# Row scores of two graph attentions by way of DRAM instead of TensorE transposes, and three steps of the turn moved

## Chip, cores and metric

The kernel runs on one core of a Trainium2 chip. The metric is the device time of one execution in microseconds (us); the time before is the median of three runs.

The engines go by the profile's short names: PE is TensorE (PEld its weight loads), DVE is VectorE, ACT is ScalarE, POOL is GpSimd, and SP is SyncE, which only issues DMAs here.

## What is computed

64 graphs of 256 nodes with 256 features pass through two layers. The first is a graph attention applied twice, then a feed-forward; the second is an attention with eight heads, weighted by relation, then a feed-forward. In the inputs `adj` holds only 0 and 1.

```python
# layer 0, on x (64, 256, 256) and adj (64, 256, 256)
def _gat(h, adj, W, a, out_features):
    Wh = jnp.matmul(h, W)
    Wh1 = jnp.matmul(Wh, a[:out_features])          # one score per node
    Wh2 = jnp.matmul(Wh, a[out_features:])          # one score per node
    e = Wh1 + jnp.swapaxes(Wh2, 1, 2)               # column + row
    e = jax.nn.leaky_relu(e, negative_slope=ALPHA)
    scores = jnp.where(adj > 0, e, NEG)
    att = jax.nn.softmax(scores, axis=1)
    return jnp.matmul(att, Wh)

h = _gat(x, adj, W1, a1, Fout)
h = _gat(h, adj, W2, a2, W2.shape[1])
h = _layernorm(x + h, g_ln1, b_ln1)
x = _layernorm(h + relu(h @ w_ff1 + b_ff1) @ w_ff2 + b_ff2, g_ln2, b_ln2)

# layer 1, on that x
scores = jnp.einsum('bhid,bhjd->bhij', q, k) / np.sqrt(dh)
attn = jax.nn.softmax(scores, axis=-1)
for r in range(Wv.shape[0]):
    out = out + jnp.einsum('bhij,bhjd->bhid', attn * (adj == r)[:, None], v_r)
x = _ln(src + out @ Wo + bo, g1, beta1)
x = _ln(x + gelu(x @ W1 + b1) @ W2 + b2, g2, beta2)
```

In `_gat` the sum of a column and a row is taken: every node's second score has to lie along the free dimension and be the same on all partitions. How this row is made is the subject of the change.

## The kernel before

**Groups and turns.** Two graphs make a group, so there are 32 groups and T = 4 blocks of 128 nodes in each. A software pipeline works on three groups at once. `turn(y_, x_, z)` (L1275) takes group y through the attention with eight heads and its feed-forward, group x = y+1 through the first layer's feed-forward, and group z = y+2 through both graph attentions. There are 32 turns; z exists in the first 30.

**Order of the work.** Inside a turn with an x, a manual schedule covers PE, SP, DVE and ACT: each of these engines runs its instructions in the order in which the Python code issues them. POOL is left to the framework's scheduler. So moving a line of code moves its instructions in the queue of every engine that they belong to. Waits between engines and for free buffers are inserted by the framework.

**Score rows.** Each projected block of a group carries two extra columns with the two scores of its nodes (`xp`, columns F+2 and F+3, for the first graph attention; `hp`, columns F and F+1, for the second). `score_rows` (L777) takes a PSUM bank and fills it with four PE transposes of one column, broadcast to 128 columns; the result is a row of 512 scores on all 128 partitions. `Softmax.raw` (L797) adds row and column on ACT (L799), `leaky` is a DVE step (L807), `exp` is on ACT (L810), `masks` multiplies with the transposed adjacency on DVE and sums (L814).

**A turn, as far as it matters here.** In PE's order:

- projections, scores, exponentials and masks of y's four *quads* (a graph and half the heads each), mixed with the steps of x's hidden layer, which have names such as `3b`, `7b`, `sb`, `4b` (digit: one of seven products of a Strassen-like scheme; letter: half of the hidden blocks). `project(z, blocks)` is the first graph attention's projection (matmuls L772, copies to `xp` by ACT L774);
- `sums(2)` and `sums(3)`: the third and fourth quads' weighted sums (L1143) and the sums of their weights `zo` (L1146). For these DVE made totals in tiles with the tag `es`, of which there are two (L1133);
- `shares(1)`: DVE transposes `zo`, takes reciprocals and multiplies (L1154 to L1163; the result is `oT`, which has the buffer of `qk`);
- `out_(0)` and `out_(1)`: the output projection of y's two graphs (`yop`, L850, added by DVE in L853), then the layer norm's moments on DVE (L865, L866) after each;
- `out(1)`, `out(2)`, `out(5)`, ...: x's output product in seven parts (class `HiddenOut`, L1027, added by DVE in L1035). Four sums of quarters of the hidden layer, s1 to s4, are made by DVE in `sums` (L1013); parts 5, 6, 7 and 3 load s1, s2, s3 and s4 as PE weights. Among these parts stand z's first softmax, then its weighted sums (`hpp`, L839, copied to `hp` by ACT in L841);
- the second half: y's second hidden layer (`second`, L938), then y's output product with the same class and again the sums s1 to s4; among its parts stand z's second softmax and its weighted sums (`ygp`, L850).

**DMA queue.** SP issues, in its own order: the moves `hT<-yt` that finish transposed features (L726, L737), the loads of the next groups (`load_x` L436, `load_rows` L441, `load_adjacency` L449) and the stores of the result (L1243).

**Adjacency.** `early_adjacency(z)` (L1177) is one DVE transpose of 32 x 32 squares, 128 x 1024 int32 (L704), of data that the load has laid out for it.

Of the kernel before, what the change touches and what calls it, by code (L numbers as in the profile page):

```python
# [9 lines left out]
F32 = mybir.dt.float32  # L10
# [6 lines left out]
P = 128  # L17
# [368 lines left out]
def narrow_path(  # L386
# [13 lines left out]
    nc = tc.nc  # L400
    B, N, F = x.shape
# [7 lines left out]
    T = G * NB  # L409
    TN = G * N  # L410
# [6 lines left out]
    const = ctx.enter_context(tc.tile_pool(name="const", bufs=1))  # L417
    io = ctx.enter_context(tc.tile_pool(name="io", bufs=2))
    work = ctx.enter_context(tc.tile_pool(name="work", bufs=2))
    psum = ctx.enter_context(tc.tile_pool(name="psum", bufs=1, space=PSUM))  # L420
    ctx.enter_context(nc.allow_non_contiguous_dma(reason="vectors, once"))

    def bank(name):
        return psum.tile([P, 512], F32, tag="g", name=name, bufs=6)
# [258 lines left out]
    rows = work.tile([P, T, 2 * F], F32, tag="v", name="rows", bufs=1)  # L683
# [17 lines left out]
    def adjacency(u, aq):  # L701

        aT = work.tile([P, T, N], I32, tag="aT", name=f"aT{u}")
        nc.vector.transpose(aT.rearrange("p t n -> p (t n)"), aq.rearrange("p t n -> p (t n)"))  # L704
        return aT
# [60 lines left out]
    def projected(u, hT, blocks, xp):  # L766
        if xp is None:
            xp = work.tile([P, T, WX], F32, tag="wh", name=f"xp{u}")
        for t in blocks:
            ps = bank(f"xpp{u}_{t}")  # L770
            for k in range(KB):
                nc.tensor.matmul(ps[:, :WX], hT[k][:, t * P:(t + 1) * P], gwe[:, k, :],  # L772
                                 start=(k == 0), stop=(k == KB - 1))
            nc.scalar.copy(xp[:, t, :], ps[:, :WX])  # L774
        return xp

    def score_rows(u, l, wh, c):  # L777

        rows = bank(f"rows{u}_{l}")
        for t in range(T):  # L780
            nc.tensor.transpose(rows[:, t * P:(t + 1) * P],  # L781
                                wh[:, t, c:c + 1].to_broadcast([P, P]), ident)
        return rows

    class Softmax:
# [46 lines left out]
    def gat_first(u, s, xp, hp=None, blocks=range(T)):  # L832
        if hp is None:
            hp = work.tile([P, T, WX], F32, tag="wh", name=f"hp{u}")
        for t in blocks:
            b, i = divmod(t, NB)
            ps = bank(f"hpp{u}_{t}")
            for j in range(NB):
                nc.tensor.matmul(ps[:, :WH], s[:, b * NB + j, i * P:(i + 1) * P],  # L839
                                 xp[:, b * NB + j, :WH], start=(j == 0), stop=(j == NB - 1))  # L840
            nc.scalar.copy(hp[:, t, :WH], ps[:, :WH])  # L841
        return hp
# [54 lines left out]
    def affine(y, g_, b_):  # L897

        times(y, g_)
        plus(y, b_)  # L900

    def times(y, g_):
        nc.vector.tensor_mul(y, y, g_[:, None, :].to_broadcast(list(y.shape)))  # L903

    def plus(y, b_):
        nc.vector.tensor_add(y, y, b_[:, None, :].to_broadcast(list(y.shape)))  # L906
# [270 lines left out]
    def early_adjacency(z):  # L1177
        g[z]["aT"] = adjacency(z, g[z]["aq"])

    def project(z, blocks=range(T)):  # L1180
        d = g[z]
        d["xp"] = projected(z, d["xT"], blocks, d.get("xp"))

    def first_scores(z):
        d = g[z]
        d["m"] = Softmax(z, 0, d["xp"], score_rows(z, 0, d["xp"], F + 2), F + 3)

    def second_scores(z):
        d = g[z]
        d["m"] = Softmax(z, 1, d["hp"], score_rows(z, 1, d["hp"], F), F + 1)  # L1190

    def first_softmax(z):
        first_scores(z)
# [8 lines left out]
    def first_sums(z, blocks=range(T)):  # L1202
        d = g[z]
        d["hp"] = gat_first(z, d["m"].s, d["xp"], None if blocks[0] == 0 else d["hp"], blocks)
# [70 lines left out]
    def turn(y_, x_, z, rest=None):  # L1275
        Y, X, Z = (g.get(u) for u in (y_, x_, z))
        hT, y = Y["hT"], Y["y"]
        quads = [(b, m) for b in range(G) for m in range(KB)]
        p = Projections(y_, hT)
# [10 lines left out]
        def powers(n, heads):  # L1290
            exps(pe[n], *e[n], heads)
# [7 lines left out]
        def sums(n):  # L1299
            b, m = quads[n]  # L1300
            if m == 0:
                acc[b] = [psum.tile([P, 512], F32, tag=t_, name=f"{t_}{y_}_{b}") for t_ in ("po", "zo")]
            applied(b, m, v, *e.pop(n), *acc[b])
# [12 lines left out]
        def first(names):  # L1316
            steps(names)

        def moved(moves, n):
            for _ in range(n):  # L1320
                nc.scalar.copy(*next(moves))
# [3 lines left out]
        with order:  # L1325
# [27 lines left out]
            if X:  # L1353
                moved(moves, 2)
                p("q6")
                moved(moves, 1)
                p("v6")
                moved(moves, 3)
                times(X["y"], rg1)
                p("q3 q7 v7")  # L1360
                while late:
                    affine(*late.pop(0))
                p("v3 q4 v4")
                plus(X["y"], rb1)
                if waiting:
                    last = norm(w, 3, wy, mv=last)
                steps = first_hidden(x_)
                scores(0)
                scores(1, ())
                first("2a")  # L1370
                powers(1, (0, 1, 2))
                masks(0, (0,))
                if waiting:
                    offsets(*last)
                first("1a")
                masks(0, (2,))
                totals(0)
                first("5a")
                powers(1, (3,))
                first("2b 3a")  # L1380
                if waiting:
                    applied_norm(wy, *last, [0, 1])
                masks(1, (0,))
                first("6a")
                masks(1, (2,))
                totals(1)
                if waiting:
                    applied_norm(wy, *last, [2, 3])
                scores(2, ())
                sums(0)  # L1390
                powers(2, range(HPB))
                sums(1)
                first("ra")
                scores(3)
                masks(2, (0,))
                if Z:
                    early(z)
                shares(0, [0])
                if not y_:
                    with behind("low"):  # L1400
                        made(w1m, 2)
                first("7a sa 1b")
                shares(0, [1])
                masks(2, (2,))
                totals(2)
                first("5b 4a 6b 3b")
                masks(3, (0,))
                if Z:
                    project(z, range(0, 1))
                first("rb 7b")  # L1410
                if Z:
                    project(z, range(1, 2))
                first("sb")
                masks(3, (2,))
                totals(3)
                sums(2)
                sums(3)
                first("4b")
            else:
                powers(0, (1,))  # L1420
                p("q3 v3")
                powers(0, (2, 3))
                p("q6 v6 q7 v7")
                with behind("projected"):
                    masks(0)
                    totals(0)
                while late:
                    affine(*late.pop(0))
                p("q4 v4")
                scores(1)  # L1430
                masks(1)
                totals(1)
                sums(0)
                piece()
                scores(2)
                sums(1)
                piece()
                with behind("out"):
                    shares(0)
                masks(2)  # L1440
                totals(2)
                scores(3)
                piece()
                piece()
                masks(3)
                totals(3)
                sums(2)
                sums(3)
            if not Z:
                shares(1)  # L1450
            if X:
                out = HiddenOut(x_, 0, X["y"], X["h1"], wf2s, out_sums(x_, 0))
                if Z:
                    out.sums(1, 2)
            if Z:
                shares(1)
            if not y_:
# [7 lines left out]
                n = norm(y_, 2, y, range(NB))  # L1465
            piece()
            if Z:
                project(z, range(T // 2, T))
            if Z:
                early_adjacency(z)  # L1470
            elif X:
                out.sums(1)
                out(1, 2)
                out.sums(2)
            out_(1)
            piece()
            if Z:
                first_scores(z)
            if Z:
                n = norm(y_, 2, y, mv=mv)  # L1480
            else:
# [51 lines left out]
                n = moments(x_, 1, X["y"], range(NB))  # L1533
            if Z:
                first_sums(z, range(T // 2, T))
            if X:
                out.product(4)
            tt = work.tile([P, HPB, NB * N], F32, tag="e", name=f"tt{y_}_1")
# [39 lines left out]
            if y_ >= NG - 2:  # L1578
# [6 lines left out]
                    for _ in pieces:  # L1585
                        pass
                return
            second_scores(z)
            out = HiddenOut(y_, 1, y, h1, w2s, out_sums(y_, 1))
            out.product(1)  # L1590
            out.sums(1, 2)
# [191 lines left out]
    c = work.tile([P, 4], F32, tag="mv", name="checks")  # L1783
# [51 lines left out]
```

## Time and profile before

| | |
|---|---|
| median of three runs | 2951.56 us (2950.34 to 2952.9) |
| the profiled execution's own time | 2950.62 us |
| its span (first to last instruction) | 2949.0 us |
| granted TensorE clock | 0.998 |
| PE, PEld, DVE busy | 2921.7, 2505.9, 2611.3 us |
| ACT, POOL busy | 1897.2, 625.6 us |
| PE transposes of score rows in the turns and the set-up (L781) | 2 x 128, mean 0.273 and 0.278 us |
| DMA traffic | 34 GB/s mean |

How to read it: the profile is one execution, so durations from it are set against 2950.62 us. A turn with all three groups repeats every 89.97 us. Matmuls are pipelined, so the mean duration of a transpose (0.27 us) is longer than the step from one to the next (0.11 us). A bracket such as `[0.33 <-PE yf L1027]` gives the idle time of an engine ahead of an instruction and what ended it; `x16` says that so many instructions in a row are shown as one line.

### The profile page before, as it was taken

The page shows a single profiled execution, that of the slowest core. Times are in us where ns is not written, and L with a number is a line of the kernel's source. Part 1 is how long each engine was busy: PE and PEld are TensorE (multiplying, and loading weights), DVE is VectorE, ACT ScalarE, POOL GpSimd, SP SyncE. Part 2 cuts the span into 40 slices and gives each one's busy share as a digit, 9 for nine tenths or more (in the row PEclk, how much of TensorE's full clock was granted, in tenths as well). Part 3 has the DMA queues.
Part 4 walks back from the last instruction along what each step waited for, and adds up shares of the span by engine and source line. Part 5 has one row for each costly group of instructions (what it writes and reads, how often), then busy time and mean ns, then how long its engine had stood idle before and what let it go on. Part 6 is the DMA issues. An engine that isn't in the chain of part 4 may idle for free.

```text
span 2949.0 us, 58651 instructions
## 1 busy us (share of the span) xinstructions
PE 2921.7 (99%) x22206; PEld 2505.9 (85%) x22206; DVE 2611.3 (89%) x5028; ACT 1897.2 (64%) x3983; POOL 625.6 (21%) x931
## 2 busy tenths in 40 slices
PE   9999999999999999999999999999999999999997
PEld 7788888888888888888888888888888888888876
DVE  5889899989899889999898998899998989988887
ACT  5566666676676666666766766766667667667652
POOL 3312221122121122221221211222212212112211
PEclk9999999999999999999999999999999999999999
DMA  5011111111111111111111111111111111111000
GB/s 152 13 30 32 39 32 32 24 40 32 37 30 26 34 34 38 33 31 24 40 32 37 31 28 31 36 36 35 29 23 40 32 37 32 28 30 33 18 8 16
DMA packets 408020, 99.27 MB, mean 34 GB/s; under 512 B 357834, under 2 KB 407220, under 8 KB 407732
## 3 DMA queue, kind: packets, MB, share of 16 engines
q1 hardware_dynamic: 406332, 94.13, 14.8%
q8 instruction: 178, 2.92, 0.4%
q0 software_dynamic: 1056, 1.05, 0.1%
q14 instruction: 110, 0.90, 0.1%
q10 hardware_dynamic: 344, 0.28, 0.0%
HBM read 56.78 MB, written 16.78 MB: 25 GB/s over the span
## 4 chain that ended last, share of the span: by engine, by line
PE 97%; DVE 2%; ACT 1%; DMA 0%; issue 0%; POOL 0%; DVEq 0%; POOLq 0%; ACTq 0%
PE yf L1027 27%; PE h1a L938 15%; PE h1b L938 11%; PE po L1143 8%; PE v L1094 6%; PE qk L1094 6%; PE sp L1115 4%; PE hpp L839 4%; PE ygp L850 4%; PE xpp L772 4%; PE yop L850 4%; PE zo L1146 2%; PE rows L781 1%; DMA first<-in_adj_dram 0%; DVE st L865 0%
## 5 line engine op out<-in xcount | busy, mean ns | idle before, releaser
L1124 ACT ACTIVATE e<-sp 128x512 f32<-128x512 f32 x512 | 271.0, 611 | 71.2 <-issue 43.7
L1128 DVE TENSOR_TENSOR ea<-e,aT 128x1024 f32<-128x1024 f32 x256 | 311.1, 1217 | 1.6 <-ACT e L1124 1.6
L894 ACT ACTIVATE y<-y,nm,rs 128x256 f32<-128x256 f32 x442 | 235.1, 592 | 64.0 <-DVE nm L884 63.2
L947 DVE TENSOR_TENSOR h<-h1a,h 128x512 f32<-128x512 f32 x293 | 197.5, 682 | 81.7 <-PE h1a L938 78.5
L950 ACT COPY h<-h1b 128x512 f32<-128x512 f32 x293 | 175.2, 599 | 124.6 <-PE h1b L938 122.8
L956 ACT ACTIVATE h<-h,cols 128x256 f32<-128x256 f32 x512 | 221.9, 502 | 35.7 <-DVE h L947 31.5
L734 POOL COPY hT<-yt 32x256 f32<-32x256 f32 x244 | 211.3, 866 | 144.8 <-DVE yt L717 132.1
L1081 ACT COPY qk<-qk 128x512 f32<-128x512 f32 x128 | 74.3, 580 | 237.4 <-PE qk L1094 236.6
L865 DVE BATCH_NORM_STATS2 st<-y 128x6 f32<-128x256 f32 x512 | 208.7, 409 | 5.7
L876 POOL TENSOR_SCALAR rs<-mv 128x4 f32<-128x4 f32 (+1 forms) x134 | 41.7, 312 | 805.1 <-DVE mv L866 438.5
L1035 DVE TENSOR_TENSOR y<-yf,y 128x256 f32<-128x256 f32 x448 | 185.9, 415 | 29.8 <-PE yf L1027 29.8
L956 ACT ACTIVATE h<-h1a,cols 128x256 f32<-128x256 f32 x256 | 102.6, 465 | 131.9 <-PE h1a L938 131.9
L1156 POOL TENSOR_TENSOR low<-low,rq 128x16 f32<-128x16 f32 x64 | 13.9, 217 | 811.6 <-DVE rq L1155 811.6
L906 DVE TENSOR_TENSOR y<-y,rb 128x1024 f32<-128x1024 f32 x126 | 163.2, 1295 | 2.2
L1133 DVE TENSOR_TENSOR es<-e 128x1024 f32<-128x1024 f32 x128 | 156.0, 1219 | 0.0
L903 DVE TENSOR_TENSOR y<-y,rg 128x1024 f32<-128x1024 f32 x126 | 153.0, 1214 | 0.0
L877 POOL TENSOR_TENSOR rs<-rs,mhalf 128x4 f32<-128x4 f32 (+1 forms) x134 | 139.5, 1041 | 8.3
L1115 PE MATMUL sp<-qk 32*128 32x256 f32 x2048 | 138.4, 394 | 0.0
L938 PE MATMUL h1a<-tt,wf 128*128 128x256 f32 x512 | 137.7, 392 | 0.0
L1143 PE MATMUL po<-e,v 128*32 128x256 f32 x2048 | 135.5, 382 | 0.0
L1143 PE MATMUL po<-ea,v 128*32 128x256 f32 x2048 | 134.5, 379 | 0.0
L717 DVE STREAM_TRANSPOSE yt<-y 128x256 f32<-128x256 f32 x364 | 128.2, 407 | 0.9 <-ACT y L894 0.7
(288 smaller groups left out, 7738.4 us busy)
## 6 DMA issues: line engine op xcount, KB each, us to landing
hT<-yt SPq DMA_DIRECT2D x666, 32.0 KB, 1.8
y<-in_x_dram SPq DMA_DIRECT2D x32, 512.0 KB, 4.1
xq<-in_x_dram SPq DMA_DIRECT2D x240, 64.0 KB, 2.3
aq<-in_adj_dram SPq DMA_DIRECT2D x240, 64.0 KB, 2.3
out_dram<-y SPq DMA_DIRECT2D x30, 512.0 KB
wf<-in_L_gnn_w_ff_dram SPq DMA_DIRECT2D x2, 1024.0 KB, 7.8
w<-in_L_gnn_W_dram SPq DMA_DIRECT2D x2, 1024.0 KB
first<-in_adj_dram POOLq DMA_DIRECT2D x2, 512.0 KB, 9.0
```

Of the source, the lines that this page charges most:

```text
L734: nc.gpsimd.tensor_copy(to, at)
L850: nc.tensor.matmul(ps[:, i * F:(i + 1) * F], lhs(t, k), rhs(b, k), start=(k == 0), stop=(k == n - 1))
L865: nc.vector.bn_stats(st[:, t, :], y[:, t, :])
L894: mark["normed"] = nc.scalar.activation(y[:, t, :], y[:, t, :], AF.Identity, bias=nm[:, t:t + 1], scale=rs[:, t:t + 1])
L938: nc.tensor.matmul(ps[:, i * N:(i + 1) * N], w_[:, f * P:(f + 1) * P], m, start=first and i == 0, stop=True, skip_group_check=True)
L956: nc.scalar.activation(y, y if ps is None else ps[:, i * N:(i + 1) * N], func, bias=bi[:, f:f + 1])
L1027: nc.tensor.matmul(s.ps[n][:, i * F2:(i + 1) * F2], a[:, k, i * P:(i + 1) * P], w_[:, k, :], start=n in (1, 2, 5) and i == 0 and k == 0, s ...
L1094: nc.tensor.matmul(ps[:, i * N:(i + 1) * N], l, r, start=n in (1, 2, 5) and i == 0, stop=True, skip_group_check=True)
L1115: nc.tensor.matmul(ps[a][:, j * N:(j + 1) * N], k_[hp, m, j0:j0 + P], q[hp, m, b * N:(b + 1) * N], start=True, stop=True)
L1124: nc.scalar.activation(e[:, a, :], ps[a], AF.Exp, scale=isd)
L1128: nc.vector.tensor_tensor(ea[:, a:a + 2, :], e[:, a:a + 2, :], ab[:, None, :].to_broadcast([P, 2, NB * N]), ALU.mult)
L1143: nc.tensor.matmul(po[hp, m * N:(m + 1) * N], vs[:, hp], w[:, a, j * N:(j + 1) * N], start=(n == 0), stop=(n == len(terms) - 1))
```

## The change

- A new function `line_rows` writes the score column of all four blocks, 512 numbers, to a line in DRAM with one DMA, and reads the line back to all 128 partitions with a second one (256 KB into SBUF). Both are on SP's queue, and the second waits for the first. The tile has the tag `es`, which the totals of the exponentials and the reciprocals have too.
- Both softmaxes of the turns take their rows from there. The set-up in front of the turns, which handles groups 0 and 1, keeps `score_rows`.
- The first attention's projection is wholly ahead of `sums(2)`: blocks 0 and 1 where block 0 stood, blocks 2 and 3 where block 1 stood. Before, blocks 2 and 3 came between `out_(0)` and `out_(1)`.
- `early_adjacency` stands ahead of `sums(3)` rather than between `out_(0)` and `out_(1)`; on DVE that is between the totals of quad 3 and s1.
- Sum s2 of x's output product stands between `out_(0)` and `out_(1)` rather than right behind s1.

```diff
+    dram = ctx.enter_context(tc.tile_pool(name="dram", bufs=2, space=bass.MemoryType.DRAM))
...
+    def line_rows(u, l, wh, c):
+
+        line = dram.tile([T, P], F32, tag="line", name=f"line{u}_{l}")
+        rows = work.tile([P, TN], F32, tag="es", name=f"rows{u}_{l}")
+        nc.sync.dma_start(line.rearrange("t p -> p t"), wh[:, :, c])
+        nc.sync.dma_start(rows, bass.AP(tensor=line.tensor, offset=line.offset, ap=[[0, P], [1, TN]]))
         return rows
...
-    def first_scores(z):
+    def first_scores(z, rows=None):
         d = g[z]
-        d["m"] = Softmax(z, 0, d["xp"], score_rows(z, 0, d["xp"], F + 2), F + 3)
-
-    def second_scores(z):
+        d["m"] = Softmax(z, 0, d["xp"], score_rows(z, 0, d["xp"], F + 2) if rows is None else rows, F + 3)
+
+    def second_scores(z, rows=None):
         d = g[z]
-        d["m"] = Softmax(z, 1, d["hp"], score_rows(z, 1, d["hp"], F), F + 1)
+        d["m"] = Softmax(z, 1, d["hp"], score_rows(z, 1, d["hp"], F) if rows is None else rows, F + 1)
...
                 if Z:
-                    project(z, range(0, 1))
+                    project(z, range(0, 2))
                 first("rb 7b")
                 if Z:
-                    project(z, range(1, 2))
+                    project(z, range(2, T))
                 first("sb")
                 masks(3, (2,))
                 totals(3)
                 sums(2)
+                if Z:
+                    rows0 = line_rows(z, 0, Z["xp"], F + 2)
+                    early_adjacency(z)
                 sums(3)
                 first("4b")
...
                 if Z:
-                    out.sums(1, 2)
+                    out.sums(1)
...
             if Z:
-                project(z, range(T // 2, T))
-            if Z:
-                early_adjacency(z)
+                out.sums(2)
             elif X:
...
             if Z:
-                first_scores(z)
+                first_scores(z, rows0)
...
             if Z:
                 first_sums(z, range(T // 2, T))
+                rows1 = line_rows(z, 1, Z["hp"], F)
...
-            second_scores(z)
+            second_scores(z, rows1)
```

More of the change, by code (lines that the diff above doesn't have):

```diff
@@ L782, in score_rows @@
                                 wh[:, t, c:c + 1].to_broadcast([P, P]), ident)
+        return rows
+    def line_rows(u, l, wh, c):
[3 more added lines that the diff above has]
+        nc.sync.dma_start(rows, bass.AP(tensor=line.tensor, offset=line.offset, ap=[[0, P], [1, TN]]))
         return rows
```

## Prediction

> **What bounds the kernel now.** I read the page first, then the line that the change deletes, then one middle turn engine by engine in the timeline. The page:
>
> ```profile
> span 2949.0 us, 58651 instructions
> PE 2921.7 (99%) x22206; PEld 2505.9 (85%) x22206; DVE 2611.3 (89%) x5028; ACT 1897.2 (64%) x3983; POOL 625.6 (21%) x931
> ...
> PE 97%; DVE 2%; ACT 1%; DMA 0%; issue 0%; POOL 0%; DVEq 0%; POOLq 0%; ACTq 0%
> ```
>
> TensorE (PE) is never idle, so taking work from it looks like pure gain. But VectorE (DVE) is 89% busy, and a share over the span does not say how late DVE's results come. The timeline of PE's weight loads (start, duration, engine, line, count):
>
> ```profile
> 1511.53 0.57 PEld L781 LDWEIGHTS rows<-ident,hp 128*128 128x128 f32 x4
> 1512.07 1.87 PEld L1027 LDWEIGHTS yf<-w,h 128*128 128x128 f32 x16
> 1513.87 1.86 PEld L1027 LDWEIGHTS yf<-w2t,eq 128*128 128x128 f32 x16
> ...
> 1571.25 1.71 PEld L850 LDWEIGHTS yop<-wo,qk 128*128 128x128 f32 x8
> 1572.98 0.57 PEld L781 LDWEIGHTS rows<-ident,xp 128*128 128x128 f32 x4
> ...
> 1582.46 1.61 PEld L839 LDWEIGHTS hpp<-xp,s 128*128 128x128 f32 x8
> 1584.09 1.97 PEld L1027 LDWEIGHTS yf<-wf,eaq 128*128 128x128 f32 x16
> ```
>
> The L781 groups go away. What matters is what stands behind them: `yf<-w2t,eq` is product 5 of the second feed-forward's output and loads the sum s1 that DVE makes; `yf<-wf,eaq` at 1584.09 is product 7 of the first one's output and loads s3. DVE's timeline of the same turn:
>
> ```profile
> 1512.53 1.23 DVE L1013 TENSOR_TENSOR eq<-h 128x1024 f32<-128x1024 f32 x1 [1.58 <-ACT h L956]
> ...
> 1566.68 1.23 DVE L1013 TENSOR_TENSOR eq<-eq,h 128x1024 f32<-128x1024 f32 x1
> 1567.82 0.71 DVE L1154 STREAM_TRANSPOSE rz<-zo 128x512 f32<-128x512 f32 x1
> ...
> 1570.21 0.68 DVE L853 TENSOR_TENSOR y<-yop,y 128x512 f32<-128x512 f32 x1
> ...
> 1572.02 1.23 DVE L704 STREAM_TRANSPOSE aT<-aq 128x1024 int32<-128x1024 int32 x1
> 1573.40 0.69 DVE L853 TENSOR_TENSOR y<-yop,y 128x512 f32<-128x512 f32 x1 [0.16 <-PE yop L850]
> ...
> 1575.62 0.42 DVE L1035 TENSOR_TENSOR y<-yf,y 128x256 f32<-128x256 f32 x1 [0.33 <-PE yf L1027]
> ...
> 1582.25 1.36 DVE L1013 TENSOR_TENSOR eaq<-h 128x1024 f32<-128x1024 f32 x1
> ```
>
> Second half: s1 ends at 1512.53+1.23 = 1513.75 and its load starts at 1513.87, 0.115 later. Read over all 30 turns that have this pair, that distance is 0.114 to 0.125 us every time: PE is already only just waiting for DVE there. First half: s3 ends at 1582.25+1.36 = 1583.61, its load at 1584.09, 0.48 later in nearly every turn; less the 0.115 that a load needs after its sum, there are 0.37 us to spare. From 1570.21 to 1583.61 DVE has no idle time but the two brackets, 0.16 and 0.33 us. So PE and DVE are both critical in a turn of 89.97 us (1512.53 to 1602.49 for the same instruction).
>
> **What the Trainium skill says.** "Perfetto Trace Analysis", Optimization Strategy: a kernel can have regimes in which the most-contended engine changes; the trace agrees (above). "DMA: Bandwidth & Descriptors", Rules for kernel authors: a strided last dimension becomes one descriptor per element, so the line's write is 512 descriptors of 4 bytes; no transfer of before is that fine. Same page, Anatomy of one DMA: some 2.0 us fixed per DMA, mostly the write's receipt, longest to HBM. The DMA table agrees for what it has: 32 KB `hT<-yt` lands in 1.8 us, 64 KB `xq` in 2.3.
>
> **The change part by part, in that turn's times.**
>
> *Removed:* four transposes twice a turn. From the first to the next product PE takes 1573.63−1573.20 = 0.43 and 1512.18−1511.74 = 0.44 us; in 30 turns 26 us of PE time, the most that can be won. ScalarE's (ACT) eight reads of the scores come from SBUF instead of PSUM; I count that as nothing, within ±0.1 us a turn, hidden by ACT's idle 1.28 us before its exponentials.
>
> *Added:* two DMAs per attention on SP's queue. First attention: the last copy of the projection is done about 1564.8 (below). Write 1.8 us (nearest row) to 8.4 (estimate: 2 us plus 32 elements per DMA engine at 0.2 us of HBM access each, from the page's Latency and other measured facts); read of 256 KB 2.3 to 4.1 (64 and 512 KB rows). I take 5 together, so the rows are there at 1570. The deadline is about 1575.9, two score reads (0.83 us) before the leaky step at 1576.76 computed below: 11 us of room, upper end 12.5. In SP's queue the next work is the four `hT<-yt` issues at 1582.16; nothing waits behind. Second attention: the copies end at 1498.4, the write queues behind the 512 KB `y` load (4.1 us), rows at about 1508.4 (1499.3+4.1+5), needed at 1513.8; the twelve `hT<-yt` behind it start at 1508.64 and their product is used at 1521. All counted as nothing; late rows are a rival.
>
> *Moved, projection:* blocks 2 and 3 (1569.72 to 1571.47: 1.75 us) go ahead of the third quad's sums. Sums 2 and 3, 4b and the first `yop` group come 1.75 later; the second `yop` does not move. ACT's two extra copies delay its `sb` step from 1564.2 to about 1565.7, still ahead of s1 at 1566.7: nothing.
>
> *Moved, adjacency and s2:* they change places on DVE, 1.23 us each: nothing by itself.
>
> *What this does to DVE:* zo's last matmul ends at 1566.48+0.61 = 1567.09 now, 1568.84 then. DVE is through with s1 at 1567.9, as before, and now idles 1 us. Reciprocal and division run 1568.88 to 1571.35; the second `yop` load, due at 1571.25, waits to 1571.46 (+0.21). The first `yop` product ends at 1567.99+1.89+1.75 = 1571.63, so its addition starts at 1571.66 instead of 1570.21: 1.45 later. From there DVE is saturated. It took 1583.61−1570.21 = 13.40 before; the two idles (0.49) go, and 0.16 more, since an instruction that waits for nothing starts some 0.08 before its predecessor's end (1582.25 against 1581.94+0.39), at two places: 12.75. The leaky step comes 0.8 later (1575.96 to 1576.76) and s3 ends at 1571.66+12.75 = 1584.41. Product 7 can load at 1584.41+0.115 = 1584.52. Unhindered PE would be there at 1584.09−0.43+0.21 = 1583.87; it waits 0.65 and is **0.43 later than before**. Behind product 7 DVE has work that PE does not need at once, and idles 0.35 before the last addition (1589.82), so it catches up there.
>
> *Second half:* PE would reach product 5 at 1513.43, but s1's chain starts from the same PE products at the turn's middle (the h1a products from 1500.5 on) through additions, norm, transposes and eight ACT steps, none of them changed. It still arrives at 1513.75. PE waits 0.44: gain 0.
>
> *Sum:* 0.43 us × 30 turns = +13 us. Against the profiled execution's own 2950.62 us that is 2963.6; the median, 2951.56, is 0.94 above it, so 2964.5.
>
> **The rivals.**
> 1. *TensorE alone counts* (faster): both sums come early enough, perhaps since DVE's stretch packs tighter. For it: 99% busy PE and no wait in PE's list but 20 us, most at the ends. Against: the constant 0.115. It decides if s3 would end before 1583.5 and s1 before 1513.3. −26 us: 2925. If only the first half gains, −13: 2938.
> 2. *Break-even:* the stretch from the first `yop` addition to s3 shrinks by some 0.4 us more than I see, or PE's stages lose less between the merged groups. Second half 0, first half 0: 2951.
> 3. *Late rows* (slower still): the round trip by DRAM takes the upper 12.5 us, ready at 1577.3, against 1575.9: 1.4 us × 30 = 42 us on top of 13, 3006. It decides from 11 us on. Against: the DMA table has 32 and 64 KB landing in 1.8 and 2.3 us, in 128 B packets.
> 4. *Buffers:* the rows share the two `es` buffers with the exponentials' totals; if the reciprocal's tile must wait for the buffer of the rows (freed by ACT only after its score reads at about 1572), division comes 1 to 3 us late: 30 to 90 us, 2995. Against: with two in turn it gets that of the fourth total, freed by sums 3.
>
> **How the numbers follow.** Stated case 0.66; faster 0.12 (rival 1 and parts of it); break-even 0.14; late rows and buffers 0.08. ±0.2% (5.9 us) is about what a measurement of this kernel can tell from no change. The stated case's own range is 0.25 to 0.75 us a turn, 2958 to 2974: the overlap term may be missing (+0.16), or the score reads may let DVE start sooner. All of it is slower by over 0.2%, so slower is 0.74, same 0.14, faster 0.12. The range leaves out most of the faster cases and the late rows: 2947 to 2978.
>
> **What would show it.** Right: L781 left with only the 16 setup transposes; PE busy about 26 us less while the span grows; in PE's waits, `yf` waiting for DVE's `eq` 0.44 and for `eaq` 0.5 to 0.7 a turn, and `yop` for DVE's `qk` 0.2; `y<-yop` on DVE preceded by an idle ended by PE; the rows landing 4 to 8 us after their write is issued, ACT's L799 no longer waiting. Wrong: no wait of PE on those sums (rival 1), or ACT waiting for a DMA ahead of L799, and DVE for it at L807 (rival 3).

## Result, and the profile after

The changed kernel takes 3069.22 us (median of five runs, 3061.36 to 3073.61) against 2951.56: ratio 1.0393, 95% interval 1.0381 to 1.0404. Slower, as forecast, but by 118 us where 13 were forecast. The profiled execution took 3070.37 us with a clock of 0.987, and the mean turn 93.65 us instead of 89.97: 110 us in 30 turns. Another 8.7 us lie ahead of the first turn with a z (121.9 us instead of 113.2), where PE ran 20.5 us at half clock instead of 3.4. How long that stretch is differs between executions (23.9 us in the profiled ones of e1_moves_only and e5_packed, 3.4 in most others) and moves a time by up to 10 us, so small differences are read below from the turns.

From the page of the kernel after (span, busy times, the shares of the chain that ended last):

```profile
span 3068.5 us, 58409 instructions
PE 2953.9 (96%) x21966; PEld 2506.9 (82%) x21966; DVE 2606.9 (85%) x5028; ACT 1905.4 (62%) x3983; POOL 621.0 (20%) x931
...
PE 71%; DVE 10%; DMA 9%; ACT 5%; issue 2%; POOL 1%; SPq 1%; DVEq 0%; ACTq 0%; POOLq 0%
```

PE had been the whole chain (97%); now DMA, DVE and ACT hold a quarter of it. PE has 240 matmuls less and is busy for longer: at half clock, at the start and in the places shown below, the same matmuls take longer. The waits, one view for each engine (us in total, times, longest), first ACT's and DVE's, then SP's queue and PE's:

```profile
ACT s L808 <- DMA rows<-line: 234.1, 43, 8.5
...
DVE s L816 <- ACT s L808: 82.0, 43, 3.5
```

```profile
SPq L791 <- DMA line<-hp: 265.7, 30, 10.6
SPq L791 <- DMA line<-xp: 243.5, 29, 10.3
```

```profile
PE yf L1036 <- DVE y L1044: 83.4, 43, 3.7
PE yf L1036 <- DVE eq L1022: 6.2, 30, 0.2
```

This is one chain read backwards. PE waits for an addition of DVE, DVE's leaky step (L816, formerly L807) for ACT's score reads, ACT for the row, and the read of the row (L791) for its own write, some 9 us each time. Not every microsecond counts: of ACT's 234 us most fell into time in which it had nothing due, and 82 reached DVE.

Before, DVE's only idle times in the same stretch of a turn were 0.16 and 0.33 us. Here is one turn of the kernel after, in the order of the chain. First SP's queue (start, duration, what is issued):

```profile
1636.39 0.38 SPq L790 DMA_DIRECT2D line<-xp  x1
1644.82 0.35 SPq L791 DMA_DIRECT2D rows<-line  x1
...
1664.87 0.36 SPq L790 DMA_DIRECT2D line<-hp  x1
1674.64 0.34 SPq L791 DMA_DIRECT2D rows<-line  x1
```

From the issue of the write to that of its read 1644.82−1636.39 = 8.43 us passed. ACT's and DVE's timelines:

```profile
1649.67 1.71 ACT L808 ACTIVATE s<-rows,xp 128x256 f32<-128x256 f32 x4 [7.33 <-DMA rows<-line]
...
1678.79 1.31 ACT L808 ACTIVATE s<-rows,hp 128x256 f32<-128x256 f32 x3 [0.57 <-DMA rows<-line]
```

```profile
1650.61 1.49 DVE L816 SCALAR_TENSOR_TENSOR s<-s 128x512 f32<-128x512 f32 x2 [2.25 <-ACT s L808]
```

The score reads start 4.85 us after the read's issue and 13.28 us after the write's. DVE stood idle for 2.25 us ahead of the leaky step. PE, in an earlier turn and then at product 5 of the second half:

```profile
1554.26 3.74 PE L1036 MATMUL yf<-wf2t,eq 128*128 128x128 f32 x32
1560.61 2.74 PE L1036 MATMUL yf<-wf,eaq 128*128 128x128 f32 x16 [2.62 <-DVE y L1044]
...
1565.91 1.95 PE L1036 MATMUL yf<-wf,eaq 128*128 128x128 f32 x16
```

```profile
1678.18 2.02 PE L1036 MATMUL yf<-w2t,eq 128*128 128x128 f32 x16 [0.20 <-DVE eq L1022]
```

The product at 1560.61 is product 3 of the first half. It uses the PSUM bank of product 5, and so waits until DVE has added product 5, which stands behind the leaky step in DVE's queue. Its 16 matmuls take 2.74 us, those at 1565.91 take 1.95. The granted clock of three neighbouring stretches shows why (bounds, length, busy time of PE and the others, PEclk):

```profile
1558.38:1561.79 3.41, 1.18 (x10) 1.18 (x11) 3.38 (x15) 2.65 (x6) 0.20 (x1) 1.00 0.00 0
1561.79:1565.20 3.41, 3.41 (x13) 3.04 (x13) 3.41 (x7) 3.34 (x9) 2.23 (x3) 0.50 0.07 19
1565.20:1568.61 3.41, 3.41 (x25) 3.16 (x25) 2.64 (x4) 3.31 (x8) 2.18 (x2) 1.00 0.22 72
```

Around such a wait the trace grants half the clock for 3.413 us, in 14 of the 30 turns with a z; the kernel before has this in none of them (each of the two has one more behind them). "TensorE: Matmul & The Clock Gate", Part 1 of the Trainium skill, describes this: a gate that halves the clock after an idle window of about 3.4 us and counts in windows of 3413 ns. The length agrees to the nanosecond, and the starts of the 14 lie whole multiples of it apart. The idle time doesn't agree: PE's waits were shorter, 2.3 to 2.9 us in 13 of the 14. What separates the turns in this trace is how a wait lies to these windows. In the window ahead of each of the 14, PE was idle for 2.02 us or more (3.41−1.18 = 2.23 in the one shown); in no other window of the turns was it idle for more than 1.94, though the other 16 turns have waits of 2.1 to 3.5 us too. The same holds for the 13 intervals in the turns of e3_line_first below (1.98 or more, and 1.94). Behind the last of these turns three intervals, in e7_packed_s2 and e10_both, follow 1.6 to 1.9 us of idle time, so this bound is not the whole rule.

### The profile page after: what moved, and what is told of

It is laid out like the page before. It is cut to its first block, busy times and chain, and to the rows that moved or that the text cites. A ratio compares the mean times of both kernels' runs of the same rounds, so it can differ in the third digit from the quotient of the medians.

```text
span 3068.5 us, 58409 instructions
## 1 busy us (share of the span) xinstructions
PE 2953.9 (96%) x21966; PEld 2506.9 (82%) x21966; DVE 2606.9 (85%) x5028; ACT 1905.4 (62%) x3983; POOL 621.0 (20%) x931
## 4 chain that ended last, share of the span: by engine, by line
PE 71%; DVE 10%; DMA 9%; ACT 5%; issue 2%; POOL 1%; SPq 1%; DVEq 0%; ACTq 0%; POOLq 0%
PE yf L1036 16%; PE h1a L947 9%; PE h1b L947 8%; PE v L1103 6%; PE qk L1103 6%; PE po L1152 6%; DMA rows<-line 5%; PE sp L1124 4%; PE hpp L848 4%; DMA line<-xp 4%; PE xpp L773 4%; PE ygp L859 4%; ACT h L965 2%; PE yop L859 2%; ACT s L808 2%
## 5 line engine op out<-in xcount | busy, mean ns | idle before, releaser
L1036 PE MATMUL yf<-wf,eaq 128*128 128x128 f32 x1024 | 143.3, 299 | 78.5 <-DVE y L1044 78.4
L1036 PEld LDWEIGHTS yf<-wf,eaq 128*128 128x128 f32 x1024 | 132.8, 208 | 92.0 <-DVE y L1044 84.3
L808 ACT ACTIVATE s<-rows,xp 128x256 f32<-128x256 f32 x128 | 54.3, 496 | 222.0 <-DMA rows<-line 221.7
L816 DVE SCALAR_TENSOR_TENSOR s<-s 128x512 f32<-128x512 f32 x128 | 87.9, 688 | 85.4 <-ACT s L808 82.0
```

The costliest lines, as they stand in the source:

```text
L1036: nc.tensor.matmul(s.ps[n][:, i * F2:(i + 1) * F2], a[:, k, i * P:(i + 1) * P], w_[:, k, :], start=n in (1, 2, 5) and i == 0 and k == 0, s ...
```

## Experiments

Comparisons are with the kernel before on the same chip. Turns are medians over a profiled execution, counted from DVE's transpose of x for the group z (`xT<-xq`, L1174 before). "First" and "second" mean the two graph attentions of a turn, or the half of a turn that holds each; the second half begins with PE's first matmul of y's second hidden layer (`h1b<-hT,w`, L938 before). Where the rows are late, turns differ from each other by up to 3 us, and the median tells less than the mean.

| kernel | first row | second row | median us | ratio, 95% interval | turn us |
|---|---|---|---|---|---|
| before | PE | PE | 2951.56 | 1 | 89.97 |
| after | line | line | 3069.22 | 1.0393 [1.0381, 1.0404] | 93.76 |
| e1_moves_only | PE | PE | 2959.25 | 1.0025 [1.0016, 1.0035] | 90.17 |
| e2_line_second | PE | line | 2979.97 | 1.0096 [1.0073, 1.0120] | 90.95 |
| e3_line_first | line | PE | 3054.60 | 1.0355 [1.0326, 1.0384] | 92.97 |
| e4_no_write | read only | read only | 2961.31 | 1.0031 [1.0018, 1.0043] | 90.17 |
| e5_packed | packed line | packed line | 2975.48 | 1.0059 [1.0036, 1.0081] | 90.39 |
| e7_packed_s2 | packed line | packed line | 2956.60 | 1.0017 [1.0007, 1.0026] | 90.02 |
| e8_packed_s2_split | packed line | packed line | 2960.35 | 1.0024 [1.0016, 1.0033] | 90.14 |
| e9_first_hoisted | packed line | PE | 2973.89 | 1.0085 [1.0069, 1.0101] | 90.57 |
| e10_both | packed line | line, early | 2972.38 | 1.0063 [1.0046, 1.0081] | 90.42 |
| e12_dense_second | PE | line, early | 2943.01 | 0.9971 [0.9961, 0.9981] | 89.56 |
| e11_packed_dense | packed line | line, early | 2937.92 | 0.9954 [0.9936, 0.9971] | 89.40 |

### Which part costs what

**e1_moves_only:** the moves stay, both rows come from PE again (against the kernel after).

```diff
-                    rows0 = line_rows(z, 0, Z["xp"], F + 2)
...
-                first_scores(z, rows0)
+                first_scores(z)
...
-                rows1 = line_rows(z, 1, Z["hp"], F)
...
-            second_scores(z, rows1)
+            second_scores(z)
```

> The changed kernel with both row scores made by TensorE transposes again; the three moved steps stay moved. Theory (the round trip through DRAM costs most, the moves cost VectorE's shorter cover): 0.43 us a turn, about 2964 us, TensorE waits some 0.2 us a turn for s3 and none for the leaky step. Rival (the moves cost it all): about 3069 us. Second rival (the moves cost nothing by themselves): 2951 us.

**e2_line_second** makes the first pair of these edits alone, **e3_line_first** the second pair alone:

```diff
 # e2
-                    rows0 = line_rows(z, 0, Z["xp"], F + 2)
-                first_scores(z, rows0)
+                first_scores(z)
 # e3
-                rows1 = line_rows(z, 1, Z["hp"], F)
-            second_scores(z, rows1)
+            second_scores(z)
```

> The changed kernel with the first attention's rows by TensorE again, the second's by the line in DRAM. Theory: 2964 us from the moves, and a late row in about half of the turns at the second attention, 0.3 to 0.5 us a turn on average, so 2970 to 2980 us; no half-speed intervals of TensorE's clock. Rival (both attentions share the loss equally): about 3015 us.

> The changed kernel with the second attention's rows by TensorE again, the first's by the line. Theory: the first attention carries nearly all of the loss: some 2.7 us a turn, and another 1.5 us in about half of the turns by a lower clock after the long wait, 3045 to 3060 us. Rival (equal shares): about 3015 us.

**e4_no_write** keeps the reads and drops the writes: the row is a piece of the input x, so the scores are other numbers, and nothing waits for a landing.

```diff
-        nc.sync.dma_start(line.rearrange("t p -> p t"), wh[:, :, c])
-        nc.sync.dma_start(rows, bass.AP(tensor=line.tensor, offset=line.offset, ap=[[0, P], [1, TN]]))
+        src = x[0:1, 0:2].rearrange("b n f -> (b n f)")
+        nc.sync.dma_start(rows, bass.AP(tensor=src.tensor, offset=src.offset, ap=[[0, P], [1, TN]]))
```

> The changed kernel without the write of the line: both rows are read by the same 256 KB transfer from a fixed line of the input x, so the scores' row part is other data and nothing waits for a write. Theory: the read alone lands in about 5 us, well ahead of its use, and what is left is the moves' cost less nothing: the sum of the prediction, about 2964 us, with waits for s1 of 0.4 us and for s3 of 0.6 us a turn, and the full clock. Rival (the read's 256 KB, or traffic on the DMA rings, costs too): above 2985 us. Rival (TensorE alone counts once the rows are early): 2925 us.

Measured side by side, with the kernel before at 2952.69: the moves cost 2959.25−2952.69 = 6.6 us, the first line 3054.60−2959.25 = 95.4, the second 2979.97−2959.25 = 20.7. Together these are 123, against 118 for the whole change. They don't simply add: in e2 the second half is 0.67 us longer than before in the mean (53.53 against 52.86), in the kernel after only 0.26, and the kernel after has its long start besides. Since e4 stands where e1 stands (both turns 90.17), what comes on top of the moves goes with the write and the wait for it; reading the rows from SBUF and the buffers of tag `es` cost nothing that shows.

PE's waits, e3 and then e4:

```profile
PE yf L1036 <- DVE y L1044: 83.2, 36, 3.4
```

```profile
PE yf L1035 <- DVE y L1043: 6.6, 7, 2.6
PE yf L1035 <- DVE eq L1021: 6.5, 30, 0.5
```

The second line of e4 is the wait of product 5 for s1 in the second half: once in each of 30 turns, with the transposes gone and no row late. Product 5 ends where it ended before (16.27 us after the middle of the turn, 16.26 before). This is why the second half gains nothing.

The first line's 95 us can be taken apart by turns. In the 17 turns of e3 without a half-speed interval the first half is 39.94 us long in the mean, against 37.33 in e1: 2.6 us for the late row, 78 us in 30 turns. In the 13 turns with one it is 41.34, 1.40 us more, 18 us in all. PE waits nearly as long in both kinds of turns (2.7 us in the mean, and 2.6), so that nearly all of the 1.40 us goes with the clock and not with a later row.

### Why the write takes 9 us

**e5_packed:** GpSimd first gathers the column into a tile of its own, so that each partition's four scores are one piece of 16 bytes: 128 pieces instead of 512. The row then lies node by node, and ACT reads every fourth number.

```diff
-        line = dram.tile([T, P], F32, tag="line", name=f"line{u}_{l}")
+        col = work.tile([P, T], F32, tag="col", name=f"col{u}_{l}")
+        line = dram.tile([P, T], F32, tag="line", name=f"line{u}_{l}")
...
-        nc.sync.dma_start(line.rearrange("t p -> p t"), wh[:, :, c])
+        nc.gpsimd.tensor_copy(col, wh[:, :, c])
+        nc.sync.dma_start(line, col)
...
-        return rows
+        return rows.rearrange("q (p t) -> q t p", t=T)
...
```

> The changed kernel, but the scores are first gathered by GpSimd into a tile of 128 x 4 and the line is written in 128 pieces of 16 bytes instead of 512 of 4 bytes; the row is read back as before and ScalarE takes it with a stride. Theory (the write's receipts come back one after another, per piece): the write lands in about 3 us instead of 8 to 10, both rows are in time, and the kernel is where the one without a write was, about 2961 us. Rival (a fixed price of a write to DRAM, whatever its pieces): still 8 us or more, above 3030 us.

**e6_probe:** the kernel before with an extra write and a small read behind it in each turn, which no other work waits for; four kinds in turn: 512 pieces of 4 bytes side by side (S = 1) or 512 bytes apart (S = P), 128 pieces of 16 bytes, 128 of 512 bytes.

```diff
...
+            S = (1, P)[kind]
+            line = dram.tile([T, P, S], F32, tag=f"line{S}", name=f"probe{kind}_{z}")
+            nc.sync.dma_start(line.rearrange("t p s -> p t s")[:, :, 0], g[z]["hp"][:, :, F])
+            nc.sync.dma_start(back[:, 0:1], line[0:1, 0, 0:1])
...
+            line = dram.tile([P, T], F32, tag="line", name=f"probe{kind}_{z}")
...
+            line = dram.tile([P, P], F32, tag="lines", name=f"probe{kind}_{z}")
...
```

> The kernel before with one extra write to DRAM a turn behind the second score column, whose landing a small read on the same queue waits for; its form changes from turn to turn: 512 pieces of 4 bytes side by side, 512 pieces of 4 bytes at 512 bytes from each other, 128 pieces of 16 bytes, 128 pieces of 512 bytes. Theory (receipts in turn, per piece): 8 to 10 us for both forms of 512 pieces, about 3 to 4 us for both forms of 128. Rival (pieces that share a memory line wait for each other): 8 to 10 us only for those side by side, and more than 4 for 128 pieces of 16 bytes. Rival (a piece below 512 bytes costs a read first): 128 of 512 bytes about 2 us, 128 of 16 bytes clearly more.

The probe left the kernel's time as it was: 2953.35 us in its one run, with turns of 89.97.

SP's waits in the probe; the first line holds both kinds of 4-byte pieces:

```profile
SPq L431 <- DMA probe<-hp: 83.8, 14, 10.2
SPq L435 <- DMA probe<-mhalf: 25.8, 8, 3.8
SPq L439 <- DMA probe<-ident: 24.0, 8, 3.3
```

Taken apart by kind, from the issue of the write to that of the read: 512 pieces of 4 bytes side by side 8.8 to 10.7 us; 512 such pieces at a spacing of 512 bytes 3.7 to 4.0; 128 of 16 bytes 3.6 to 4.3; 128 of 512 bytes 2.6 to 3.9. All four were issued 0.4 to 0.6 us behind y's load of 512 KB, so the three shorter times may be this load's as much as their own. The theory that each small piece costs its own receipt falls: the same 512 pieces, spaced, land in less than half the time. For pieces of 4 bytes it counts that they lie side by side. The 16-byte pieces lie side by side too and are not slow, which the rival had not expected (more than 4 us); whether their size or their smaller number helps them was not tried. "DMA: Bandwidth & Descriptors", Specifications, of the Trainium skill says that transfers below 512 bytes are read-modify-write; pieces that share the same 512 bytes would then have to follow one another, 128 of them in the 4-byte line and 32 in the 16-byte line. That is a guess which fits the probe; no run here shows it.

In e5 the lines land in time (write to read 1.7 us in the first half, median), and the first half is as long as e4's. Yet e5's profiled execution is 16 us longer than e4's (2976.24 against 2960.22). Its longer stretch at half clock at the start is 10 of these; what remains is the price of the strided read. Score reads, e5 and then the kernel after (busy, mean ns of one):

```profile
L811 ACT ACTIVATE s<-rows,hp 128x256 f32<-128x256 f32 x120 | 82.5, 770 | 0.0
L811 ACT ACTIVATE s<-rows,xp 128x256 f32<-128x256 f32 x120 | 81.9, 755 | 20.6 <-DMA rows<-line 20.6
```

```profile
L808 ACT ACTIVATE s<-rows,xp 128x256 f32<-128x256 f32 x128 | 54.3, 496 | 222.0 <-DMA rows<-line 221.7 <-PE rows L782 0.3
```

That is a quarter of a microsecond more for each of eight reads in a turn; the second half is 0.22 us longer than e4's, 7 us in 30 turns.

### Can the moves and the second half be made to pay?

**e7_packed_s2:** as e5, with s2 of x's product back behind s1.

```diff
-                    out.sums(1)
+                    out.sums(1, 2)
...
-            if Z:
-                out.sums(2)
-            elif X:
+            if not Z and X:
```

> As the packed version, with s2 back behind s1 ahead of the reciprocals, so that VectorE does it in the idle time in front of zo. Theory: VectorE's stretch behind the first yop product is 1.14 us shorter, the wait for s3 goes and the first half gains 0.3 to 0.44 us a turn against before; the second half still waits for s1: about 2940 us (2937 to 2944). Rival (zo is not what VectorE waits for, or another wait takes its place): 2952 us or more.

DVE then makes s2 in the 1 us in which it waits for `zo`. The forecast of 2940 us was missed. The first half is 36.98 us against 37.33 in e5 and 37.13 before: a gain at last, but of 0.15 us rather than the transposes' 0.43; the second `yop` group now starts 0.21 us later than before, behind the division, which takes most of the rest. The second half gives 0.2 back.

**e8_packed_s2_split:** s1 of the second half also in two pieces, so that product 5 starts on the first.

```diff
...
+                if n == 1 and split:
+                    for k in (slice(0, 2), slice(2, 4)):
+                        mark["quarters"] = nc.vector.tensor_tensor(o[:, k], x_[:, k], y_[:, k], op)
+                    continue
...
-            out.sums(1, 2)
+            out.sums(1, split=True)
+            out.sums(2)
```

> As the one with s2 ahead, and the second feed-forward's s1 made in two halves, of which the first needs only the first half of ScalarE's steps, so that its last part ends some 0.5 us earlier. Theory (the second half waits for s1 alone): both deletions of transposes now count, 0.8 us a turn, about 2928 us (2924 to 2934). Rival (another chain of the second half is as long): no better than the one without the split, about 2940 us.

The forecast of 2928 us was missed too. The wait for s1 is gone and another has its place, at product 7 (PE's timeline):

```profile
1526.91 2.05 PE L1047 MATMUL yf<-w,eaq 128*128 128x128 f32 x16 [0.38 <-DVE y L1055]
```

By the timelines, ACT's strided reads (2.75 us for four) make DVE's leaky step late, and with it the addition of product 6, whose bank product 7 takes.

**e9_first_hoisted:** e7's first half with x's product 1, its addition, z's score reads and exponentials moved up between the two `yop` groups; the second row from PE.

```diff
             if Z:
-                out.sums(2)
+                first_scores(z, rows0)
+                out(1)
+                Z["m"].scores(0)
...
             out_(1)
...
```

> The first attention by the line in 16-byte pieces with s2 ahead of the reciprocals; the second by TensorE's transposes as before; and x's first output product with its addition, and z's leaky steps and exponentials, between the two yop groups, so that the second yop group does not wait for the division. Theory: the first half now shows the deleted 0.43 us in full, the second half is that of before: about 2940 us. Rival (VectorE's stretch is as long as TensorE's, since the moments of the second graph come later): 2948 us or more.

The forecast of 2940 us was missed by 34. Compared with e7, the second `yop` group starts 1.57 us later, behind the product that was moved ahead of it (20.76 us after the turn's start instead of 19.19). Its addition follows at 22.69, and everything behind it on DVE: s3 ends at 32.26 instead of 30.97.

**e10_both:** e9's first half; in the second the 4-byte line of the changed kernel, but written ahead of y's load on SP's queue and read behind it, with s1 in two pieces.

```diff
-                rows1 = line_rows(z, 1, Z["hp"], F)
+                read1 = dense_rows(z, 1, Z["hp"], F)
+                if z + 1 < NG:
+                    load_rows(z + 1)
+                rows1 = read1()
```

> As the one before, and the second attention by a line of 4-byte pieces too, whose write is issued ahead of the load of y so that its row comes without a stride and in time (13.5 us after the write, with some 15 us of room), and s1 of the second feed-forward in two halves. Theory (in the second half only s1, late rows and the slow strided read stood in the way): another 0.4 us a turn, about 2928 us. Rival (the row is late, or the next chain, the addition ahead of part 7, holds TensorE): no better than without, 2940 us or more.

The whole disappoints as e9 does, but from the middle of the turn to the next turn's start it needs 0.33 us less than the kernel before (median). So its second half was put behind other first halves: **e12_dense_second** behind that of before, **e11_packed_dense** behind that of e7 (edits as in e10 and e7, without e9's).

```diff
 # e11 and e12, second half
+                read1 = dense_rows(z, 1, Z["hp"], F)
+                if z + 1 < NG:
+                    load_rows(z + 1)
+                rows1 = read1()
...
+            out.sums(1, split=True)
 # e11 alone, first half
+                    rows0 = line_rows(z, 0, Z["xp"], F + 2)
...
+                    out.sums(1, 2)
```

> First half as before (x's rows transposed, nothing moved), second half as e10_both alone. If the second half gains 0.36 us by itself: turn 89.6 us, 30 x 0.36 = 11 us under before, 2941 us, ratio 0.9963. If that gain was borrowed from e10_both's first half: turn 90.0 us, 2952 us, ratio 1.000. If the line is late, over 91 us a turn and over 2980 us.

> First half of the turn as e7_packed_s2 (x's rows by the packed line, s2 ahead of the reciprocals, nothing hoisted), second half as e10_both (hp's rows by 512 pieces of 4 bytes, written ahead of y's load, s1 in two halves). If the halves add: turn 90.0 - 0.15 (first half of e7_packed_s2 against before) - 0.36 (second half of e10_both against before) = 89.46 us, some 15 us less than before over 30 turns, 2937 us, ratio 0.995. The rival, that the shorter second half was only e10_both's own first half paying back (work that lay ahead there), gives a second half like e7_packed_s2's or before's: turn 89.8 to 90.0, 2948 to 2956 us. If hp's line lands later than its read is wanted, as in the kernel after: a turn over 91 us and over 2980 us.

Both gains stood, and by the turns they added. The second half takes 89.56−37.13 = 52.43 us in e12 and 89.40−36.98 = 52.42 in e11, against 52.84 in the kernel before and in e4: 0.41 of the 0.44 us of the transposes. SP's queue in e12:

```profile
1493.57 0.39 SPq L800 DMA_DIRECT2D dense<-hp  x1
1494.49 0.37 SPq L442 DMA_DIRECT2D y<-in_x_dram  x1
1503.93 0.34 SPq L803 DMA_DIRECT2D rows<-dense  x1
```

The write still takes 8.3 to 11.4 us. It is issued 0.4 us after the start of the last copy of `hp` instead of 1.7 (medians), and the score reads wait at most 0.16 us for the row. So it is the lateness of the row that costs, not the write itself or SP's queue standing behind it. PE's timeline no longer has a bracket at product 5:

```profile
1506.84 1.95 PE L1059 MATMUL yf<-w,h 128*128 128x128 f32 x16
1508.62 1.95 PE L1059 MATMUL yf<-w2t,eq 128*128 128x128 f32 x16
```

And the page of e11, to be set beside that of before: PE's busy time is 16.5 us less, and the span 12.6.

```profile
span 2936.4 us, 58412 instructions
PE 2905.2 (99%) x21966; PEld 2475.9 (84%) x21966; DVE 2616.5 (89%) x5058; ACT 1931.4 (66%) x3983; POOL 662.6 (23%) x961
```

e11, at 2937.92 us, beats both kernels, the one before by 0.5%. The split alone, with the transposes kept, was not run; at product 5 it has nothing to take away, since the matmuls of product 5 start 1.78 us after those of product 1 before as well as in e12 (in e4, which waits, 2.16).

## Why the prediction was right or wrong

**The step that failed** is *Added*: "I take 5 together". The working gave the write 1.8 to 8.4 us, and the sum took the low end, from transfers of 128-byte packets. Measured for the first line: 8.5 us for the write (median, 8.2 to 10.8) and about 5 for the read, 13.3 from the issue of the write to the first score read. The deadline that the text had worked out, 11 us of room, held: 13.3−11 = 2.3 us late, and e3's first halves without a half-speed interval are 2.3 (shortest) to 2.6 us (mean) longer than e1's. The right arithmetic was there with the wrong value in it; rival 3 was what happened, with the sign that the text had named for it (ACT waiting for a DMA, and DVE for ACT), and the chance of 0.08 that it shared with the buffers was an error of the same step.

**Luck.** That the kernel became slower was forecast, but for a reason that makes up 6.6 of the 118 us; that both reasons point the same way is luck. And the upper estimate of the write, 8.4 us, is near the measured 8.5 by luck: 32 elements at 0.2 us each, one after another, would hold for spaced pieces too, and these took 3.7 to 4.0. Its 2 us of fixed cost are given in the cited section for DMAs that GpSimd issues; these came from SP's queue.

**Rival 3's price** was too small as well: 42 us for a round trip of 12.5 us, where 13.3 came, 2.3 to 2.6 us a turn. It left out that the second line would be late too (20.7 us by itself), and that PE, kept waiting, runs at half clock around the wait (18 us in e3).

**The moves** (forecast +13, measured 6.6): the working of DVE's queue was right to a few hundredths, read from e4 in us after the turn's start. The forecast of the second row follows from the prediction's steps without being stated there.

| event | forecast | e4 |
|---|---|---|
| addition of the first `yop` starts | 19.17 | 19.18 |
| addition of the second `yop` | 22.12 | 22.10 |
| leaky step | 24.27 | 24.21 |
| s3 ends | 31.92 | 31.86 |
| load of product 7 | 32.03 | 31.91 |

The size was off at the end. The load of product 7 follows s3 by 0.05 us, not by the 0.115 read in the second half, so it is 0.31 us later than before (31.60) instead of 0.43. And a load is not yet a product: before, the matmuls of product 7 began 0.22 us behind their first load, now they begin with it. So product 7 ends 0.20 us later than before (33.97 against 33.77), and the second half starts 0.20 us late (37.33 against 37.13). For the same reason the second `yop` lost little: its load came 0.25 us later than before, behind the division, about as forecast, but its matmuls only 0.06. In e7, where the division ends 0.15 us later, they came 0.21 later.

**The second half, gain 0:** right, and shown by e4 (product 5 waits for s1 in 30 of 30 turns) and by e12, where breaking that wait brings the gain. Only "already only just waiting" was too strong for the kernel before: its s1 came just in time, and product 5 wasn't held up.

**Buffers (rival 4):** nothing of it shows; e4 and e1 agree. **ACT's reads from SBUF**, counted as nothing within 0.1 us a turn: one follows the other by 0.40 us instead of 0.36 from PSUM, 0.34 us for eight, and that too was hidden. **TensorE alone counts (rival 1):** of its 26 us, e11 gets 14, and the change as it was made gets none.

## What to carry to other kernels

A round trip through DRAM on a tight path has to be priced by the form of its smallest piece: if the nearest row of the profile has other pieces, take the upper estimate for the deadline test, and issue the write as early as its data allow. Here work taken from a saturated engine paid only where no result of another engine arrived just in time behind it; find that arrival first and split or move it, then take the work away. PE, made to wait, also lost clock, which no sum of waits contains.

## What was not expected of the hardware

- 512 writes of 4 bytes side by side in DRAM took 8.2 to 11.7 us until a dependent read was issued, over all runs; at 512 bytes from each other 3.7 to 4.0. The packets themselves were over within 0.4 us (1637.31 to 1637.69 in the turn shown); it is the completions that come late, 6.4 to 8.3 us after the issue in that turn and 5.9 to 9.5 in the next.
- ACT's score read of 128x256 float32 from SBUF took 0.76 us on average at a stride of 16 bytes, and 0.50 side by side.
- PE ran at half clock for 3.413 us where it had been idle for about 2.0 us or more within one of a fixed row of windows of that length (27 intervals in the turns of two kernels); waits of the same size that fell across two windows left the clock alone.
- In PE's queue the load of product 7 started 0.05 us after the end of s3, for which it waited; the load of product 5 started 0.115 us after s1, and that of `yop` 0.11 us after the division.
